# A planner's due times, allowances and forced work in a four-layer Mamba and convolution kernel

## The chip, the cores and the metric

The kernel runs on one core of one Trainium2 chip, in one launch. The metric is the device time of one execution in microseconds (us); below, the median of three runs. The core's engines work from instruction queues of their own: PE multiplies matrices (its weight loads are PEld), DVE does vector work, ACT evaluates functions, POOL does further vector work, and SP issues the DMA transfers here. All data are 32-bit floats.

## The reference

The input x is 8 images of 384 channels and 32 x 32 pixels. Four layers follow one another; each normalizes x over groups of 12 channels and adds its result to x.

```
x = x + mamba(group_norm(x))                # layer 0, "l0_"
x = x + frequency_mixer(group_norm(x))      # layer 1
x = x + mlp(mamba(layer_norm(group_norm(x))))   # layer 2, "l2_"
x = x + depthwise_3x3(group_norm(x))        # layer 3

def mamba(x):                    # per image, over 1024 pixels in order
    xin, z = split(x @ in_proj.T)               # 768 channels each
    u = silu(causal_conv3(xin))
    dt, Bm, Cm = split(u @ x_proj.T)            # 24, 16, 16 columns
    dt = softplus(dt @ dt_proj.T + bias)
    h[t] = exp(dt[t] * A) * h[t-1] + dt[t] * u[t] * Bm[t]   # 768 x 16 states
    y[t] = sum over states of h[t] * Cm[t]
    return ((y + u * D) * silu(z)) @ out_proj.T
```

Layer 1 multiplies by a 384 x 384 matrix, filters the frequencies of 8 x 8 patches, convolves 3 x 3 per channel, multiplies one half of the channels with the Gelu of the other and projects back. The mlp of layer 2 widens 384 channels to 1536, takes Gelu, and comes back.

## The kernel before

**Chunks and steps.** A Mamba layer is cut in chunks of half an image, T = 512 pixels. Layer 0 has chunks n = 0 to 15, layer 2 chunks 16 to 31; the even chunk is an image's first half (c = 0), the odd one the second. Layers 1 and 3 need both halves, so they run once per pair of chunks. A chunk has NQ = 24 steps, one for 32 of the 768 channels and their 16 states: 768 steps in all, numbered t, and i within a chunk. The loop over t (L1007) writes the engines' queues in this order for a step:

- `times` (L619, POOL) multiplies the next step's input g by B: two products of 128 x 1024.
- `scan` (L637) runs this step's four recurrences on DVE, two of them with a product by C after; POOL takes the product of the other two (L660).
- `jobs.begin` (L124) gives the step its allowance, and `jobs.step(t, 2.0)` runs a first part of the side work.
- `gather` (L664, PE) sums the states of the step before into y; every fourth step adds u * D and DVE multiplies by the gate z.
- `begin` (L610, SP) starts the load of g for the step AHEAD = 3 on; it needs that step's "dud", which the side work makes.
- `jobs.step(t)` (L133) runs more side work, and `decay` (L627) makes the next step's exp(dt * A): four matmuls into four PSUM banks, four Exp on ACT. They overwrite the banks which this step's scans read.

[...]PE comes to the next `decay` only after the side work put ahead of it, and DVE to the next scan only after the side work's DVE operations.

**Jobs.** All else is side work in generators, cut in pieces by their `yield`:

- `gates(s, h)` (L440): the gate z of half h of the channels, needed at i = 12h + 4.
- `front(s)` (L487): loads and normalizes x, in_proj, the convolution, x_proj, then dt and dud for six blocks of channels. Block 0 of the next chunk is needed at i = 21, block k at step 4k - 3 of that chunk.
- `measure(s)` (L399): group statistics of the next image, by two buffers "spm" that `front` uses too.
- `out_proj(s)` (L681): the output projection; in layer 2 it also starts the loads of the mlp's weights mw (four buffers). Called from `finish(s)` (L717), which goes on with `mlp(s)` (L891) in layer 2. Then comes `layer1` (L796) or `layer3` (L962), once per pair.

Their PSUM results go through NBANK = 3 banks (`pipe`, L189).

**The planner** (`Jobs`, L88) decides in Python, as the program is written, which piece goes where. It books a piece's PE time as columns/600 us and its DVE time as 0.1 + columns/830 us per operation (by the output's columns, L71). A job has a first step and a due step ("last"). In `step` the pieces are tried by due time, and one is put in if the step's rooms for PE and DVE (`ROOM`, L68) hold what the job's piece of that number took last time, less 0.1. A piece that ends with NEXT stops its job for this step; one that ends with EARLY stops it until `begin` of the next step, which runs one such job's next piece ahead of all else (a long Silu or Gelu). WAIT means that something isn't there yet. `begin` carries what is left of a room into the next step: at most an eighth of the room as a gain, at most the room as a debt. `until` (L148) is the force: where a step can't go on without a result, it runs pieces by due time, without regard to rooms, until the result is there. It is called for the gates (L1021), for the dud (L1035) and at the end (L1042).

Of the kernel before, what the change touches and what calls it, by code (L numbers as in the profile page):

```python
# [17 lines left out]
B, C, H, W = 8, 384, 32, 32  # L18
L = H * W
KC = C // P  # L20
# [7 lines left out]
NCH = L // T  # L28
# [12 lines left out]
NSUB = 4  # L41
NQ = ND * NSUB
QUADS = [(k, s) for k in range(ND) for s in range(NSUB)]
NH = ND // 2
# [20 lines left out]
NEXT = "next"  # L65
EARLY = "early"

ROOM = {"l0_": (5.2, 3.0), "turn": (6.4, 3.0), "l2_": (6.4, 3.0)}  # L68


class Meter:  # L71
# [18 lines left out]
class Jobs:  # L90
# [42 lines left out]
    def step(self, t, most=None):  # L133

        most = most and self.work[0] + most
        went = True
        while went and not (most and self.work[0] >= most):
            went = False
            for job in self.in_order():
                need = self.need(job)  # L140
                if job["got"] is None and job["first"] <= t and all(
                    y == 0 or x >= y - 0.1 for x, y in zip(self.room, need)
                ):
                    went = self.piece(job)
                    if went:
                        break

    def until(self, done):  # L148

        while not done():  # L150
            if not any(self.piece(job) for job in self.in_order()):
                raise RuntimeError("no job goes on")


# [1 line left out]
def tile_conv_preact_d4(ctx: ExitStack, tc: tile.TileContext, a: dict, out: bass.AP):  # L156
# [10 lines left out]
    live = {"ps": 0, "dt": 0, "x": 0, "spm": False}  # L167
    work = [0.0, 0.0]
    jobs = Jobs(work)
    vector = Meter(nc.vector, work, 1)  # L170
# [109 lines left out]
    def group_stats(block, all_read=lambda: None, between=None):  # L280
# [3 lines left out]
        for h in range(2):  # L284
            for k in range(KC):
                v, then = block(h, k)
                vector.bn_stats(st[:, k, h, :], v)
                then()
                if h == 1 and k == KC - 1:
                    all_read()  # L290
                yield between
        for k in range(KC):
            vector.bn_aggr(mv[:, k, :], _flat(st[:, k]))
        yield NEXT
# [104 lines left out]
    def measure(s):  # L399

        blocks = [(h, k) for h in range(2) for k in range(KC)]
        loaded = {}

        def load(q):
            if q < len(blocks):
                h, k = blocks[q]
                x = loaded[h, k] = wk.tile([P, T], F32, tag="spm", name="xk", bufs=2)
                nc.sync.dma_start(
                    x, s["src"][s["b"], k * P : (k + 1) * P, h * T : (h + 1) * T]
                )  # L410

        live["spm"] = True
        load(0)
        load(1)
        yield NEXT

        def block(h, k):
            return loaded.pop((h, k)), lambda: load(blocks.index((h, k)) + 2)

        def all_read():  # L420
            live["spm"] = False

        s["stats"] = yield from group_stats(block, all_read, NEXT)

# [62 lines left out]
    def front(s):  # L487

        c, n = s["c"], s["n"]
        while n > 0 and ("gates", 1) not in chunks[n - 1]:  # L490
            yield WAIT
        xn = s["xn"] = load_half(s)
        if n % (B * NCH) == 0:
# [53 lines left out]
            act(_flat(uh[h]), _flat(uh[h]), AF.Silu)  # L547
        exp_again()
        yield NEXT
        ps = yield from ps_tile("ps_x")  # L550
        for d in range(ND):
            mm(ps[:RX, :], w["x"][:, d, :], u[d], start=d == 0, stop=d == ND - 1)
# [52 lines left out]
        while flying:  # L605
            flying = [f for f in flying if next(f, f) is not f]
            yield NEXT


    def begin(s, i):  # L610
# [70 lines left out]
    def out_proj(s):  # L681
# [31 lines left out]

        yield from pipe(("ps_out", stages(m)) for m in range(KC))
        s["free"] = True

    def finish(s):  # L717

        yield from out_proj(s)
        t = NQ * s["n"]  # L720
        if s["n"] == B * NCH - 1:
            load_out(layer_w["l2_"], "l2_")
        if s["pre"] == "l2_":
            yield from mlp(s)
        s["ended"] = True
        if s["pre"] == "l2_":
            if s["c"] == NCH - 1:
                jobs.add("layer3", layer3(s), 0, t + 3 * NQ - 1)
        elif s["c"] == NCH - 1:
            until = 2 * NQ + 3 if s["n"] == B * NCH - 1 else 3 * NQ - 2  # L730
            jobs.add("layer1", layer1(s), 0, t + until)

    p2 = None

# [272 lines left out]
    for t in range(total):  # L1007
# [1 line left out]
        n = s["n"]  # L1009
        later = chunks[n + 1] if n + 1 < len(chunks) else None  # L1010
        if i == 0:
            jobs.add("gates", gates(s, 1), t + 1, t + 8)
            if s["c"] == 0 and n + NCH < len(chunks):
                jobs.add("measure", measure(chunks[n + NCH]), t, t + NQ + 4)
            if later:
                jobs.add("front%d" % (later["pre"] == "l2_"), front(later), t + 3, t + 14)
                jobs.add("gates", gates(later, 0), t + 13, t + NQ + 2)
        if i == 3 and n == B * NCH:
            load_diagonal(s["w"], s["pre"])
        if i % (NH * NSUB) == NSUB:  # L1020
            jobs.until(lambda: ("gates", i // (NH * NSUB)) in s)  # L1021
        if t + 1 < total:
            times(*steps[t + 1])
        scan(s, i)
# [2 lines left out]
        if t > 0:  # L1027
            p, q = steps[t - 1]
            gather(p, q)
            if q == NQ - 1:  # L1030
                end = 10 if p["pre"] == "l0_" else 23 if p["c"] == 0 else 16
                jobs.add("end%d" % (p["pre"] == "l2_"), finish(p), t + 1, t + end)
        if t + AHEAD < total:
            p, q = steps[t + AHEAD]
            jobs.until(lambda: p.get("dud", {}).get(QUADS[q][0]))  # L1035
            begin(p, q)
        jobs.step(t)
        if t + 1 < total:
# [134 lines left out]
```

## Time and profile before

| | |
|---|---|
| median of 3 runs | 7943.07 us (7934.12 to 7946.89) |
| the profiled execution | 7942.61 us, its span 7940.8 us |
| mean granted PE clock | 0.919 |
| busy share of PE, DVE, ACT, POOL | 92%, 72%, 51%, 71% |
| DMA | 1122.90 MB, mean 141 GB/s |
| start to first scan | 92.4 us |
| chunks 0 to 15 (layer 0) | 92.4 to 3574.4 us |
| chunks 16 to 20 | 3574.4 to 4980.2 us |
| chunks 21 to 31 | 4980.2 to 7748.3 us |
| after the last scan | 192.5 us |

Steps and chunks are read off the DVE timeline: four scans are one step, and a step lasts from its first scan to the next step's first. A busy matmul in this profile may be a waiting one (its end is modelled), so PE's share overstates its work. "Idle before" names what an engine waited for. In the table of stretches the columns are the engines' busy us with their instructions, then the granted clock, the DMA share and GB/s.

### The profile page before, as it was taken

The page shows a single profiled execution, that of the slowest core. Times are in us where ns is not written, and L with a number is a line of the kernel's source. Part 1 is how long each engine was busy: PE and PEld are TensorE (multiplying, and loading weights), DVE is VectorE, ACT ScalarE, POOL GpSimd, SP SyncE. Part 2 cuts the span into 40 slices and gives each one's busy share as a digit, 9 for nine tenths or more (in the row PEclk, how much of TensorE's full clock was granted, in tenths as well). Part 3 has the DMA queues.
Part 4 walks back from the last instruction along what each step waited for, and adds up shares of the span by engine and source line. Part 5 has one row for each costly group of instructions (what it writes and reads, how often), then busy time and mean ns, then how long its engine had stood idle before and what let it go on. Part 6 is the DMA issues. An engine that isn't in the chain of part 4 may idle for free. (4 is left out here: it accounts for less than half of the span.)

```text
span 7940.8 us, 76871 instructions
## 1 busy us (share of the span) xinstructions
PE 7334.3 (92%) x25954; PEld 3037.2 (38%) x25954; DVE 5717.7 (72%) x7254; ACT 4052.0 (51%) x6980; POOL 5639.5 (71%) x2710
## 2 busy tenths in 40 slices
PE   7989999999998999989999989999899989999898
PEld 2223333333333333333334444444444444344445
DVE  5988788878787878778737647767767676676770
ACT  4445545555555555554544545555555555555553
POOL 5888888877787878777737746767767667676770
PEclk8888888989898999989889989999999999999999
DMA  5665655555564656556526645666656666565662
GB/s 138 148 148 137 144 135 136 134 133 137 133 149 118 146 129 143 122 141 151 122 69 173 159 121 144 154 158 165 157 134 163 166 149 159 138 171 140 168 157 65
DMA packets 289704, 1122.90 MB, mean 141 GB/s; under 512 B 37402, under 2 KB 91754, under 8 KB 191004
## 3 DMA queue, kind: packets, MB, share of 16 engines
q1 hardware_dynamic: 289308, 1117.98, 57.2%
q8 instruction: 205, 3.36, 0.2%
q14 instruction: 191, 1.56, 0.1%
HBM read 1042.34 MB, written 75.50 MB: 141 GB/s over the span
## 5 line engine op out<-in xcount | busy, mean ns | idle before, releaser
L623 POOL TENSOR_TENSOR g<-g,bc 128x1024 f32<-128x1024 f32 x1536 | 3586.5, 2357 | 181.3 <-DMA g<-dud 164.4
L660 POOL TENSOR_TENSOR g<-g,bc 128x1024 f32<-128x1024 f32 x768 | 1805.8, 2351 | 1609.5 <-DVE carry L656 871.8
L241 ACT ACTIVATE dA<-dA,w_A 128x512 f32<-128x512 f32 x3072 | 1858.3, 661 | 1480.3 <-PE dA L177 1467.3
L177 PE MATMUL dA<-dt,selr 32*128 32x512 f32 x6144 | 1521.9, 676 | 67.8 <-DVE g L654 59.2
L643 DVE TENSOR_TENSOR_SCAN dA<-dA,carry,g 128x512 f32<-128x512 f32 x768 | 986.7, 1285 | 750.5 <-issue 375.4
L643 DVE TENSOR_TENSOR_SCAN dA<-dA,g 128x512 f32<-128x512 f32 x768 | 940.8, 1225 | 554.3 <-ACT dA L241 221.6
L654 DVE TENSOR_TENSOR g<-dA,bc 128x512 f32<-128x512 f32 x1536 | 1054.5, 687 | 29.8 <-DVE dA L643 0.5
L177 PE MATMUL y<-g,sely 128*32 128x512 f32 x6144 | 934.2, 640 | 47.6 <-POOL g L660 42.4
L643 DVE TENSOR_TENSOR_SCAN g<-dA,carry,g 128x512 f32<-128x512 f32 x768 | 940.4, 1266 | 0.0
L643 DVE TENSOR_TENSOR_SCAN g<-dA,g 128x512 f32<-128x512 f32 x768 | 893.7, 1206 | 0.0
L177 PEld LDWEIGHTS dA<-dt,selr 32*128 32x128 f32 x6144 | 452.1, 192 | 947.2 <-DVE g L643 473.9
L177 PE MATMUL ps_up<-t,mw 128*128 128x256 f32 x2304 | 605.4, 411 | 144.4 <-ACT h L241 100.5
L177 PE MATMUL ps_dn<-h,mw 128*128 128x256 f32 x2304 | 566.1, 397 | 67.7 <-DMA mw<-in_l_mlp_w 55.9
L177 PE MATMUL ps_z<-xf,w_in 128*128 128x512 f32 x1152 | 590.0, 653 | 27.8 <-DVE dt L85 24.0
L177 PE MATMUL ps_dw<-tp,diag 96*96 96x512 f32 x1152 | 580.7, 645 | 14.3 <-ACT diag L241 14.3
L177 PEld LDWEIGHTS ps_up<-t,mw 128*128 128x128 f32 x2304 | 444.9, 201 | 371.0 <-ACT h L241 186.7
L177 PE MATMUL ps_in<-xf,w_in 128*128 128x512 f32 x1152 | 556.2, 623 | 25.3 <-DVE u L85 22.0
L177 PE MATMUL ps_out<-u,w_out 128*128 128x512 f32 x1152 | 548.7, 623 | 9.1 <-DVE x L85 9.1
L177 PEld LDWEIGHTS ps_dn<-h,mw 128*128 128x128 f32 x2304 | 436.7, 196 | 260.3 <-issue 121.0
L177 PE MATMUL ps_dw<-xp,diag 128*128 128x512 f32 x864 | 405.4, 620 | 41.0 <-ACT diag L241 40.9
L241 ACT ACTIVATE h<-ps_up,vec 128x256 f32<-128x256 f32 x384 | 177.3, 474 | 442.7 <-PE ps_up L177 442.4
L241 ACT ACTIVATE u<-ps_in,w_vec 128x512 f32<-128x512 f32 x192 | 149.4, 778 | 478.1 <-PE ps_in L177 478.1
(98 smaller groups left out, 6514.5 us busy)
## 6 DMA issues: line engine op xcount, KB each, us to landing
g<-dud SPq DMA_DIRECT2D x768, 1024.0 KB, 7.1
mw<-in_l_mlp_w SPq DMA_DIRECT2D x384, 384.0 KB, 7.2
dud<-du SPq DMA_DIRECT2D x768, 64.0 KB, 1.7
xk<-in_x SPq DMA_DIRECT2D x48, 256.0 KB, 4.1
xf<-in_x SPq DMA_DIRECT2D x16, 768.0 KB, 8.5
x<-in_x SPq DMA_DIRECT2D x16, 768.0 KB, 8.4
x_mid<-x SPq DMA_DIRECT2D x16, 768.0 KB, 4.7
xk<-x_mid SPq DMA_DIRECT2D x48, 256.0 KB, 5.4
```

Source lines behind the costliest of these rows:

```text
L177: nc.tensor.matmul(out_, lhsT, rhs, start=start, stop=stop)
L241: nc.scalar.activation(out_, in_, func, **kw)
L623: nc.gpsimd.tensor_mul(g, g, s["bc"][:, 0, :].unsqueeze(1).to_broadcast([P, 2, T]))
L643: nc.vector.tensor_tensor_scan(dAs[j] if j < own else g[:, j, :], dAs[j], g[:, j, :], 0.0 if s["c"] == 0 else carry[:, q : q + 1], ALU.mul ...
L654: nc.vector.tensor_mul(g[:, j, :], dAs[j], s["bc"][:, 1, :])
L660: nc.gpsimd.tensor_mul(g, g, s["bc"][:, 1, :].unsqueeze(1).to_broadcast([P, 4 - own, T]))
```

## The change

All of it is in the planner and in the jobs' due times; the computation stays as it is.

- `until` takes a kind of job, and tries jobs of that kind before all others. The two forced places name what they need: "gates0" or "gates1" (two kinds now), and "front0" or "front1".
- `step` lets a piece exceed the room by 0.8 where it was 0.1. DVE's room is 2.4 for 3.0, PE's in layer 2 6.5 for 6.4.
- The output projection is a job of its own ("out0", "out1"); the rest of `finish` ("end0", "end1") is added when it is done.
- All due times are new; `measure` starts at step 11 of a chunk, not 0. Every operation of `bn_stats` is booked 0.6 us more on DVE, and of six blocks of an image's means every second one ends with NEXT, not each.
- New waits of the planner: `measure` waits for the spm buffers, `front` for its statistics and, before x_proj, for the end of the front before ("spread").

```diff
-ROOM = {"l0_": (5.2, 3.0), "turn": (6.4, 3.0), "l2_": (6.4, 3.0)}
+ROOM = {"l0_": (5.2, 2.4), "turn": (6.5, 2.4), "l2_": (6.5, 2.4)}
...
-                    y == 0 or x >= y - 0.1 for x, y in zip(self.room, need)
+                    y == 0 or x >= y - 0.8 for x, y in zip(self.room, need)
...
-    def until(self, done):
+    def until(self, done, kind=None):
         while not done():
-            if not any(self.piece(job) for job in self.in_order()):
+            late = [job for job in self.in_order() if job["kind"] == kind]
+            if not any(self.piece(job) for job in late + self.in_order()):
                 raise RuntimeError("no job goes on")
...
                 vector.bn_stats(st[:, k, h, :], v)
+                work[1] += 0.6
                 then()
...
-                yield between
+                yield between if (h * KC + k) % 2 else None
...
-        live["spm"] = True
+        while live["spm"]:
+            yield WAIT
+        live["spm"] = 2
...
-        while n > 0 and ("gates", 1) not in chunks[n - 1]:
+        while n > 0 and ("gates", 1) not in chunks[n - 1] or "stats" not in chunks[n - c]:
             yield WAIT
...
+        while n > 0 and "spread" not in chunks[n - 1]:
+            yield WAIT
         ps = yield from ps_tile("ps_x")
...
         s["free"] = True
+        jobs.add("end%d" % last, finish(s), 0, NQ * (s["n"] + 1) + 18)

     def finish(s):
-        yield from out_proj(s)
...
-                jobs.add("layer3", layer3(s), 0, t + 3 * NQ - 1)
+                jobs.add("layer3", layer3(s), 0, t + 2 * NQ + 14)
         elif s["c"] == NCH - 1:
-            until = 2 * NQ + 3 if s["n"] == B * NCH - 1 else 3 * NQ - 2
-            jobs.add("layer1", layer1(s), 0, t + until)
+            jobs.add("layer1", layer1(s), 0, t + NQ + 8)
...
         if i == 0:
-            jobs.add("gates", gates(s, 1), t + 1, t + 8)
-            if s["c"] == 0 and n + NCH < len(chunks):
-                jobs.add("measure", measure(chunks[n + NCH]), t, t + NQ + 4)
+            jobs.add("gates1", gates(s, 1), t + 1, t + 4)
             if later:
-                jobs.add("front%d" % (later["pre"] == "l2_"), front(later), t + 3, t + 14)
-                jobs.add("gates", gates(later, 0), t + 13, t + NQ + 2)
+                jobs.add("front%d" % (later["pre"] == "l2_"), front(later), t + 2, t + 6)
+                jobs.add("gates0", gates(later, 0), t + 13, t + NQ - 3)
+        if i == 11 and s["c"] == 0 and n + NCH < len(chunks):
+            jobs.add("measure", measure(chunks[n + NCH]), t, t + 1)
...
         if i % (NH * NSUB) == NSUB:
-            jobs.until(lambda: ("gates", i // (NH * NSUB)) in s)
+            h = i // (NH * NSUB)
+            jobs.until(lambda: ("gates", h) in s, "gates%d" % h)
...
             if q == NQ - 1:
-                end = 10 if p["pre"] == "l0_" else 23 if p["c"] == 0 else 16
-                jobs.add("end%d" % (p["pre"] == "l2_"), finish(p), t + 1, t + end)
+                jobs.add("out%d" % (p["pre"] == "l2_"), out_proj(p), t + 1, t + 3)
...
-            jobs.until(lambda: p.get("dud", {}).get(QUADS[q][0]))
+            jobs.until(
+                lambda: p.get("dud", {}).get(QUADS[q][0]), "front%d" % (p["pre"] == "l2_")
+            )
...
-    jobs.add("end1", finish(steps[-1][0]), 0, total)
+    jobs.add("out1", out_proj(steps[-1][0]), 0, total)
```

More of the change, by code (lines that the diff above doesn't have):

```diff
@@ L165, in tile_conv_preact_d4 @@
     psy = ctx.enter_context(tc.tile_pool(name="psy", bufs=1, space=PSUM))
-    live = {"ps": 0, "dt": 0, "x": 0, "spm": False}
+    live = {"ps": 0, "dt": 0, "x": 0, "spm": 0}
     work = [0.0, 0.0]
@@ L420, in all_read @@
         def all_read():
-            live["spm"] = False
+            live["spm"] = 0
         s["stats"] = yield from group_stats(block, all_read, NEXT)
@@ L607, in front @@
             yield NEXT
+        s["spread"] = True
     def begin(s, i):
```

## The prediction

> **What bounds the kernel now.** I read the page first, for the engines' shares.
>
> ```profile
> PE 7334.3 (92%) x25954; PEld 3037.2 (38%) x25954; DVE 5717.7 (72%) x7254; ACT 4052.0 (51%) x6980; POOL 5639.5 (71%) x2710
> ...
> PEclk8888888989898999989889989999999999999999
> ...
> L623 POOL TENSOR_TENSOR g<-g,bc 128x1024 f32<-128x1024 f32 x1536 | 3586.5, 2357 | 181.3 <-DMA g<-dud 164.4
> L660 POOL TENSOR_TENSOR g<-g,bc 128x1024 f32<-128x1024 f32 x768 | 1805.8, 2351 | 1609.5 <-DVE carry L656 871.8
> ```
>
> PE looks full, but a "busy" matmul may be one that stands waiting. POOL owes every scan step three products, 3 x 2.35 = 7.1 us: a step's floor. For PE's real need I use the chain of waits, where 36 half-records of ps_dw (18 matmuls of 512 columns) take 15.72 us, 0.87 us each; the planner books 512/600 = 0.85. Below, "PE" amounts are in those booked us. In the timeline the four dA matmuls of a step take 1.14 us, the four y 1.06, D 1.13 every fourth step: 2.3 PE per step besides the jobs.
>
> Second, the busy time in stretches, one per chunk (24 steps): chunks 12, 13, 17, 20, 22, 23.
>
> ```profile
> 2676.30:2908.60 232.30, 220.25 (x750) 75.31 (x749) 184.38 (x270) 115.47 (x218) 175.25 (x88) 0.93 0.54 130
> 2908.60:3116.60 208.00, 194.23 (x669) 71.44 (x668) 171.78 (x182) 120.02 (x214) 176.68 (x83) 0.91 0.60 144
> 3817.20:4149.60 332.40, 305.59 (x906) 117.76 (x905) 179.23 (x193) 160.05 (x306) 175.96 (x84) 0.89 0.39 95
> 4667.30:4980.20 312.90, 281.92 (x1091) 145.81 (x1090) 185.21 (x270) 150.95 (x247) 176.68 (x88) 0.94 0.57 147
> 5230.40:5490.40 260.00, 241.37 (x913) 108.74 (x912) 180.58 (x266) 142.40 (x240) 175.41 (x87) 0.97 0.59 148
> 5490.40:5740.70 250.30, 225.32 (x918) 112.34 (x918) 175.82 (x192) 125.80 (x204) 176.99 (x85) 0.95 0.64 162
> ```
>
> Columns: stretch, length, busy us of PE, weight loads, DVE, ACT, POOL, granted clock. DVE and POOL need 172 to 185 us in every chunk; the length above that comes from PE. Layer 0 owes 64,512 matmul columns of job work per chunk (its half of layer 1 included), 107.5 PE, so (107.5 + 24 x 2.3)/0.92 = 177 us: PE and POOL level. Layer 2 owes 88,576 columns, 147.6 PE, so (147.6 + 55)/0.955 = 212 us: PE bounds it.
>
> Third, the DVE timeline of the longest step (chunk 17, step 21).
>
> ```profile
> 4006.17 2.45 DVE L643 TENSOR_TENSOR_SCAN g<-dA,carry,g 128x512 f32<-128x512 f32 x2
> 4022.46 0.69 DVE L85 TENSOR_TENSOR gate<-ps_dw,gate 96x512 f32<-96x512 f32 x1 [13.84 <-PE ps_dw L177]
> ...
> 4066.15 0.69 DVE L85 TENSOR_TENSOR gate<-ps_dw,gate 96x512 f32<-96x512 f32 x1 [29.94 <-PE ps_dw L177]
> ...
> 4128.80 0.69 DVE L85 SCALAR_TENSOR_TENSOR dt<-ps_dt,spm 128x512 f32<-128x512 f32 x1 [14.38 <-ACT spm L241]
> ...
> 4131.22 1.29 DVE L643 TENSOR_TENSOR_SCAN dA<-dA,carry,g 128x512 f32<-128x512 f32 x1
> ```
>
> No scan starts for 123 us: until (L148) forces the front's first dud, and all of layer 1 and an output projection, due earlier, go first. Between first scans the step is 128.9 us. Adding the planner's prices, 102 PE are in it: (102 + 2.3)/0.89 = 117. So a forced lump is mostly honest PE work, 12 us dearer than that. Smaller ones: 33.4 us (21.3 PE) at step 21 of chunks 12 and 14, 37.0 in 16, 70.3 before step 4 of chunk 20, 35.4 there in 22, 24 ... 30.
>
> Fourth, PE outside lumps, in chunk 23.
>
> ```profile
> 5623.17 1.07 PE L177 MATMUL y<-g,sely 128*32 128x512 f32 x8
> 5629.00 5.44 PE L177 MATMUL ps_up<-t,mw 128*128 128x256 f32 x12 [4.76 <-ACT h L241]
> ```
>
> PE stands 4.76 us while ACT does two table loads of 1.28 us and a long Silu. Such events leave chunk 23 at 250 us where (137.4 + 55)/0.95 = 203 would do.
>
> **What the Trainium skill says.** "Perfetto Trace Analysis", Identifying the Most-Contended Engine: matmul busy share is no measure of closeness to the limit. The trace agrees: 225 us busy for a need of 203 in chunk 23. "TensorE: Matmul & The Clock Gate", Part 1, Architectural detail: ACT and DVE queues are strictly first in, first out. The lumps agree: the next scan sits behind the forced evictions. "ScalarE: Activation LUTs", What ACT_TABLE_LOAD costs: 1283 ns a load; the trace has 1283. No page bears on the planner.
>
> **The change part by part.** No matmul, activation, scan or weight is added; the order changes. The new waits are the planner's (spread, stats, spm), so no engine queues behind them. What moves on SP's queue: x (768 KB, 8.4 us) and four mw loads (7.2 us each) with the projection, and measure's six xk (4 to 5 us) from steps 0-10 to 11-14. They pass g loads, issued three steps (25 us) ahead and landing in 7.1: hidden; uncovered, at most 8 us per chunk. Two statistics per step cost DVE 2 x 0.68 instead of one, in three steps instead of six: zero in sum. Layer statistics, six in one step before (booked 0.11 each, really 0.68; that step took 13.3 us in chunk 12), now spread: 1 to 2 us per pair, inside the rounding.
>
> *Layer 0.* I follow the new dues by hand. Even chunk: projection (15.4 PE), gates1 (7.7), front (27.3), done about step 14; layer 1's patches, one stage a step (NEXT), about step 9 to step 2 of the odd chunk. Odd chunk: layer 1 is overdue, so first: its depthwise part, 72 PE at two 2.56 pieces a step, fills steps 3 to 19 (before, it did this in steps 1-16 of the even chunk). The projection gets in at its two EARLY gaps, gates1 is forced at 16, and the front begins its matmuls at step 20 and is forced at 21 with some 19 PE: the 33.4 us lump again, in the other chunk. "Forced alone" doesn't help, it was alone in chunk 12 too. So every pair looks like chunks 12+13: 232.3 + 208.0 = 440.3 us, against a mean for chunks 2 to 15 of (3574.4 - 490.0)/7 = 440.6. Priced by classes of steps from before (up to 2 PE 7.5 us, 2 to 4.2 8.45, about 5.1 9.1, the lump 31) my list gives 449. I take 0 for layer 0; ends -60 and +60.
>
> What does change: all 215 PE of each pair are done within it. Before, chunks 0-15 did 1537 PE; the new order does 100.7 + 7 x 215 = 1606. Some 70 fewer are owed at the turn.
>
> *The turn, chunks 16 to 20.* Before: 4980.2 - 3574.4 = 1405.8 us with 762 job PE. Following the dues: chunk 16 does 90 (latency-bound), 17 134, 18 to 20 154 each at the room's pace: 686, leaving the same owed after chunk 20. (686 + 5 x 55)/0.93 = 1033, plus 45 us of stalls a chunk (what chunks 21-30 show on average is 40) = 225, plus 25 because chunk 16 is at POOL's floor: 1283. I take -120. Gates forced alone are evicted by ACT, not DVE, so scans aren't behind them.
>
> *Layer 2 steady, chunks 21 on.* Room 6.5 and slack 0.8 make steps of three 2.56 pieces (7.68) and two (5.12) alternate. The even chunks' 35.4 us lump goes, but it held 25.6 + 5.1 + 2.3 = 33 PE: nothing is gained by spreading it. By classes of before, 7 to 8 PE cost a median 12.7 us, 5.12 9.1: ten heavy and fourteen light give 254.4, against a mean of 254.4 for chunks 21 to 30. I take 0; ends -90 and +110.
>
> *Tail.* 192.5 us, with 22 PE of the previous pair's layer 3 leading it; that fits before the end now: -22/0.95 = -23, -3 of gaps in its chain, +18 paid in spare room earlier: -8.
>
> Sum on the profiled 7940.8 (92.4 to the first scan unchanged): 0 - 120 + 0 - 8 = 7813; the run has 2 us more outside the span, and its 7942.61 is the median's 7943.07 within 0.5: 7815.
>
> **The rivals.** *Smoothing pays.* In layer 2 the two-piece front steps take 9.2 us because DVE (6.2 scan + 2.9 taps) ends last, PE idling 1.5; a third piece rides free. Heavy steps at 11.5: 115 + 14 x 9.42 (class mean) = 247, -7.5 x 11 chunks = -82, and 4 us per layer 0 pair from the earlier x load (DVE stood 9.10 us for x in step 316): 7705. Against: steps of 7 to 8 PE took a median 12.7 before.
>
> *Heavy steps stall: slower.* The third piece needs one of three PSUM banks, whose evictions stand behind ACT's Gelu and Silu (4.76 us above; PE waited 88.2 us for h in 4400:7748). At 14.0 us a heavy step, a chunk is 140 + 132 = 272, +17.5 x 11 = +192: 8007. It decides from 13.4 us on: (254.4 + 128/11 - 131.9)/10.
>
> *It does nothing.* Lumps in seven odd chunks of layer 0 (the +60 end) and front lumps in 17 to 19 of the old size give back the turn: 7935.
>
> **How the numbers follow.** Forecast 0.42 (own range 7760 to 7870), smoothing 0.28, heavy steps 0.20, nothing 0.10. A measurement of this kernel tells 0.2% (16 us). Faster: 0.42 + 0.28 + 0.02 of the last; same 0.06; slower 0.20 + 0.02. Range 7640 to 7985: smoothing's centre less its unknown (-65), up to most of the +110 and +60 ends together; the far part of heavy steps stays out.
>
> **What would show it.** Right: no gap over 60 us between scans; chunks 16-20 near 1285 us; no 35 us lump at step 3 of even layer 2 chunks; a lump of some 30 us at step 21 of odd layer 0 chunks. Wrong: layer 0 pairs off 440 by over 10, or layer 2 pairs off 509 by over 15.

## The result and the profile after

The changed kernel takes 8043.76 us (median of 4 runs, 8024.73 to 8049.89) against 7944.98 us before (median of four runs now): a ratio of 1.0121, with a 95% interval of 1.01 to 1.0143. It is slower by some 1.2%. The forecast was 7815 us, in a range of 7640 to 7985. The profiled execution took 8049.89 us, its span 8048.1 us at a mean granted clock of 0.912, against 7940.8 us at 0.919: 107.3 us more.

| stretch (first scan to first scan) | before | after | difference | forecast |
|---|---|---|---|---|
| start, and chunks 0 and 1 | 490.0 | 498.2 | +8.2 | 0 |
| chunks 2 to 15 | 3084.4 | 3136.8 | +52.4 | 0 |
| chunks 16 to 20 (the turn) | 1405.8 | 1288.7 | -117.1 | -120 |
| chunks 21 to 30 | 2543.4 | 2717.0 | +173.6 | 0 |
| chunk 31 | 224.6 | 234.0 | +9.4 | +18, here or earlier |
| after the last scan | 192.6 | 173.3 | -19.3 | -26 |

The forecast's -8 for the tail is -26 at the end and +18 for the same work paid earlier; the two measured rows give -9.9. So the turn and the tail did what was forecast. The loss lies in layer 2's steady part, and a smaller one in layer 0. The page of the kernel after, by the same lines as before (the code has moved: L623 is L630 now, L660 is L667, L643 is L650):

```profile
PE 7281.8 (90%) x25954; PEld 3030.2 (38%) x25954; DVE 5765.3 (72%) x7254; ACT 4045.9 (50%) x6980; POOL 5633.0 (70%) x2710
...
PEclk8789989898989999898889999998989999999999
...
L630 POOL TENSOR_TENSOR g<-g,bc 128x1024 f32<-128x1024 f32 x1536 | 3581.8, 2353 | 173.4 <-DMA g<-dud 148.8
L667 POOL TENSOR_TENSOR g<-g,bc 128x1024 f32<-128x1024 f32 x768 | 1803.9, 2349 | 1803.9 <-DVE g L650 963.1
```

The instructions are the same in number on every engine, and POOL's products last as long as before. PE is busy for 53 us less in a span that is 107 us longer, so it stands idle more. The busy time in stretches of the kernel after, chunks 12, 13, 17, 20, 22 and 23 as before, and then chunks 2 to 15, 16 to 20 and 21 to 30 (columns as in the prediction: length, busy us of PE, weight loads, DVE, ACT, POOL, granted clock, and then DMA share and GB/s):

```profile
2733.80:2951.60 217.80, 202.13 (x712) 78.19 (x712) 190.77 (x272) 120.01 (x208) 179.94 (x95) 0.89 0.61 147
2951.60:3174.20 222.60, 210.11 (x706) 68.42 (x705) 171.01 (x179) 116.11 (x224) 172.04 (x76) 0.95 0.52 126
3859.80:4129.90 270.10, 247.45 (x767) 86.95 (x766) 173.12 (x182) 131.81 (x246) 175.94 (x78) 0.89 0.48 115
4655.00:4923.80 268.80, 241.40 (x948) 121.08 (x945) 179.56 (x265) 128.77 (x204) 178.12 (x89) 0.91 0.60 155
5190.90:5466.30 275.40, 246.55 (x994) 128.85 (x993) 179.53 (x265) 127.41 (x199) 178.89 (x89) 0.91 0.63 159
5466.30:5731.20 264.90, 237.93 (x891) 105.41 (x891) 179.75 (x197) 142.82 (x248) 172.89 (x82) 0.94 0.55 139
498.20:3635.00 3136.80, 2922.36 (x9914) 1037.45 (x9910) 2541.07 (x3154) 1649.38 (x3007) 2459.90 (x1181) 0.91 0.56 134
3635.00:4923.80 1288.80, 1169.87 (x4318) 523.28 (x4317) 906.16 (x1181) 655.34 (x1106) 880.61 (x427) 0.91 0.58 145
4923.80:7640.80 2717.00, 2403.57 (x9221) 1143.79 (x9221) 1781.37 (x2276) 1355.77 (x2227) 1767.82 (x847) 0.93 0.58 146
```

The last three stretches in the kernel before:

```profile
490.00:3574.40 3084.40, 2924.42 (x9739) 1032.04 (x9736) 2483.98 (x3148) 1628.03 (x2930) 2464.30 (x1184) 0.90 0.57 136
3574.40:4980.20 1405.80, 1285.31 (x4531) 565.88 (x4530) 907.70 (x1190) 693.22 (x1197) 882.08 (x426) 0.92 0.54 135
4980.20:7523.70 2543.50, 2331.67 (x9114) 1103.02 (x9113) 1777.37 (x2272) 1339.80 (x2208) 1761.70 (x843) 0.96 0.62 155
```

In chunks 21 to 30 the length less PE's busy time is 211.8 us before and 313.4 us after: 102 us more of idling. PE's busy time rises by 72 us as well, for 1% more records; the granted clock there falls from 0.96 to 0.93. DVE and POOL are as busy as before. So the 173 us show on PE: it waits more, and it is busy longer for nearly the same work.

The longest step of the kernel before, 128.9 us, was in chunk 17, step 21. The DVE timeline of the same step of the kernel after:

```profile
4079.93 2.95 DVE L85 SCALAR_TENSOR_TENSOR u<-ps_in,w_vec,u 128x511 f32<-128x511 f32 x4
4086.95 1.53 DVE L85 SCALAR_TENSOR_TENSOR u<-ps_in,w_vec,u 128x511 f32<-128x511 f32 x2 [4.07 <-ACT xt L242]
...
4105.21 0.69 DVE L85 SCALAR_TENSOR_TENSOR dt<-ps_dt,spm 128x512 f32<-128x512 f32 x1 [14.09 <-ACT spm L242]
...
4107.62 1.29 DVE L650 TENSOR_TENSOR_SCAN dA<-dA,carry,g 128x512 f32<-128x512 f32 x1
```

Only the front itself is forced now, and the step takes 33.9 us. The work that made the long step isn't gone: the planner put layer 1 and the projection into earlier steps. What that is worth at the turn, a_layer1_late measures below. The PE timeline of chunk 23, step 7, where a step of the steady part took 19.8 us:

```profile
5541.99 1.56 PE L178 MATMUL ps_up<-t,mw 128*128 128x256 f32 x6
5551.37 5.49 PE L178 MATMUL ps_up<-t,mw 128*128 128x256 f32 x12 [7.82 <-ACT h L242]
5556.79 1.23 PE L178 MATMUL y<-g,sely 128*32 128x512 f32 x8
5557.95 2.86 PE L178 MATMUL ps_up<-t,mw 128*128 128x256 f32 x12
```

PE stands 7.82 us because ACT does two table loads, the gates' long Silu and layer 3's xp and diag before it comes to the h that frees a bank. Then twelve ps_up records take 5.49 us; a little later twelve of the same take 2.86. The granted clock was 0.50 for the first twelve:

```profile
5546.90:5557.20 10.30, 5.83 (x16) 4.08 (x20) 2.23 (x2) 5.18 (x10) 6.95 (x3) 0.50 0.12 38
```

This idle stretch is paid for twice. The Trainium skill, "TensorE: Matmul & The Clock Gate", Why this matters for your kernels, says that gaps of more than some 3 us between matmul bursts throw the clock back to half; these records agree with it. The last section shows where the clock fell without such a gap. In chunks 21 to 30, PE has 26 idle stretches of over 3 us before (101.6 us in all) and 41 after (191.7 us).

### The profile page after: what moved, and what is told of

Read it like the earlier page. It is cut to its first block, busy times and chain, and to the rows that moved or that the text cites. A ratio compares the mean times of both kernels' runs of the same rounds, so it can differ in the third digit from the quotient of the medians.

```text
span 8048.1 us, 76877 instructions
## 1 busy us (share of the span) xinstructions
PE 7281.8 (90%) x25954; PEld 3030.2 (38%) x25954; DVE 5765.3 (72%) x7254; ACT 4045.9 (50%) x6980; POOL 5633.0 (70%) x2710
## 5 line engine op out<-in xcount | busy, mean ns | idle before, releaser
L630 POOL TENSOR_TENSOR g<-g,bc 128x1024 f32<-128x1024 f32 x1536 | 3581.8, 2353 | 173.4 <-DMA g<-dud 148.8
L667 POOL TENSOR_TENSOR g<-g,bc 128x1024 f32<-128x1024 f32 x768 | 1803.9, 2349 | 1803.9 <-DVE g L650 963.1
L650 DVE TENSOR_TENSOR_SCAN dA<-dA,carry,g 128x512 f32<-128x512 f32 x768 | 986.9, 1285 | 730.0 <-issue 309.0
L178 PE MATMUL dA<-dt,selr 32*128 32x512 f32 x6144 | 1432.3, 692 | 58.9 <-DVE g L661 55.3
L650 DVE TENSOR_TENSOR_SCAN dA<-dA,g 128x512 f32<-128x512 f32 x768 | 939.9, 1224 | 707.0 <-ACT dA L242 267.5
L650 DVE TENSOR_TENSOR_SCAN g<-dA,carry,g 128x512 f32<-128x512 f32 x768 | 940.3, 1266 | 0.0
L650 DVE TENSOR_TENSOR_SCAN g<-dA,g 128x512 f32<-128x512 f32 x768 | 893.6, 1206 | 0.0
L178 PEld LDWEIGHTS dA<-dt,selr 32*128 32x128 f32 x6144 | 428.1, 196 | 892.7 <-DVE g L650 401.8
L178 PE MATMUL ps_in<-xf,w_in 128*128 128x512 f32 x1152 | 583.5, 648 | 52.5 <-DVE u L85 50.3
L178 PE MATMUL ps_dw<-tp,diag 96*96 96x512 f32 x1152 | 546.9, 612 | 9.4 <-ACT diag L242 9.4
L178 PE MATMUL ps_dw<-xp,diag 128*128 128x512 f32 x864 | 431.0, 643 | 61.1 <-ACT diag L242 52.6
L178 PEld LDWEIGHTS y<-g,sely 128*32 128x32 f32 x6144 | 133.2, 110 | 682.4 <-issue 414.6
```

Source lines behind the costliest of these rows:

```text
L178: nc.tensor.matmul(out_, lhsT, rhs, start=start, stop=stop)
L630: nc.gpsimd.tensor_mul(g, g, s["bc"][:, 0, :].unsqueeze(1).to_broadcast([P, 2, T]))
L650: nc.vector.tensor_tensor_scan(dAs[j] if j < own else g[:, j, :], dAs[j], g[:, j, :], 0.0 if s["c"] == 0 else carry[:, q : q + 1], ALU.mul ...
L667: nc.gpsimd.tensor_mul(g, g, s["bc"][:, 1, :].unsqueeze(1).to_broadcast([P, 4 - own, T]))
```

## The experiments

The amounts called "booked PE" are the planner's own: matmul columns over 600 for the pieces that it put into the steps. Names with a_ are edits of the kernel after, names with b_ edits of the kernel before. Each ratio is to executions of the kernel before taken beside it. The runs by stretch, from the one profiled execution of each (us; booked PE of chunks 21 to 30 in the last column):

| kernel | median, ratio to before | 2 to 15 | 16 to 20 | 21 to 30 | chunk 31 and tail | booked |
|---|---|---|---|---|---|---|
| before | 7944.98 | 3084.4 | 1405.8 | 2543.4 | 417.2 | 1476 |
| after | 8043.76, 1.0121 | 3136.8 | 1288.7 | 2717.0 | 407.3 | 1503 |
| b_slack | 7835.96, 0.9864 | 2991.3 | 1342.4 | 2585.6 | 417.5 | 1475 |
| a_slack_l0 | 7938.43, 1.0001 | 3143.3 | 1270.1 | 2557.4 | 469.9 | 1461 |
| a_means_l2 | 7961.00, 1.0022 | 3143.1 | 1220.4 | 2688.9 | 405.4 | 1501 |
| a_layer1_late | 8000.22, 1.0077 | 3002.1 | 1376.7 | 2707.7 | 406.2 | 1503 |
| a_old_dues | 8009.15, 1.0085 | 3128.7 | 1372.2 | 2583.0 | 415.2 | 1492 |
| a_layer3_late | 8169.33, 1.0283 | 3130.5 | 1294.4 | 2798.0 | 438.6 | 1484 |
| a_old_rooms | 8070.32, 1.0165 | 3169.0 | 1249.8 | 2701.3 | 435.1 | 1482 |
| a_old_front | 7952.71, 1.0001 | 3174.3 | 1223.9 | 2651.8 | 407.7 | 1504 |
| a_old_ends | 7917.42, 0.9968 | 3167.8 | 1268.3 | 2546.2 | 436.1 | 1476 |
| a_old_front_ends | 8005.50, 1.0073 | 3253.6 | 1251.8 | 2558.1 | 442.7 | 1477 |
| a_old_end | 8067.12, 1.0149 | 3142.9 | 1296.6 | 2696.1 | 438.0 | 1479 |
| a_old_out | 7889.41, 0.9920 | 3171.1 | 1266.4 | 2544.9 | 410.7 | 1503 |
| a_old_ends_layer1 | 7861.20, 0.9889 | 3045.7 | 1342.7 | 2545.7 | 439.6 | 1476 |
| b_force | 8145.76, 1.0248 | 3078.0 | 1380.4 | 2730.1 | 468.6 | 1476 |
| b_slack_force | 7779.23, 0.9794 | 2970.5 | 1294.7 | 2567.8 | 438.6 | 1474 |

How far such a stretch repeats can be read from the table: after, a_slack_l0, a_means_l2, a_layer3_late and a_old_end have the same pieces in the same steps of layer 0, and took 3130.5 to 3143.3 us; after and a_layer1_late have the same in chunks 21 to 30, and took 2717.0 and 2707.7. A difference of some 13 us tells nothing.

### Slack, means and layer 1

The first theory was the rival of the prediction that came nearest to the measured time: heavy steps (three pieces), which slack 0.8 makes, stall. Its opponent was that the order of the jobs costs, and slack little. The slack alone, in the kernel before:

```
-                    y == 0 or x >= y - 0.1 for x, y in zip(self.room, need)
+                    y == 0 or x >= y - 0.8 for x, y in zip(self.room, need)
```

> The kernel before with the slack of the rooms at 0.8 instead of 0.1 and nothing else. By the planner's arithmetic, chunks 21 to 30 then hold 75 steps of more than 7 PE (10 before, 87 in the changed kernel), no forced lump at step 3, and layer 2's due times and the means stay as before. Theory 'heavy steps stall' (a third 2.56 piece in a step is what costs): chunks 21 to 30 take about 2690 us instead of 2543 (75/87 of the +173 measured). Theory 'order' (the new due times put the gates and the output projection where the mlp's pieces meet their Silu, and the means where they meet the layer norm): they take 2520 to 2560. The turn (chunks 16 to 20) has 744 PE for 762 and its forced lump 58 for 99: about 1370 us either way. Layer 0 (chunks 2 to 15) within 30 us of 3084.

Chunks 21 to 30 took 2585.6 us, 42 more than before at the same booked work, with 75 heavy steps for 10: outside both ranges, nearer to the second. Layer 0 won 93 us, which neither theory had. The whole is faster by 1.4% (0.9864, interval 0.9845 to 0.9884). So slack alone isn't the loss, and heavy steps as such are not: they lasted 11.46 us on average.

The slack taken back in the kernel after, from chunk 17 on:

```
-                    y == 0 or x >= y - 0.8 for x, y in zip(self.room, need)
+                    y == 0 or x >= y - self.slack for x, y in zip(self.room, need)
...
+        jobs.slack = 0.8 if n <= B * NCH else 0.1
         jobs.begin(ROOM
```

> The changed kernel with the slack back at 0.1 from chunk 17 on, 0.8 kept in layer 0. Steps of more than 7 PE in chunks 21 to 30 fall from 87 to 9; the work that no longer fits is forced instead, 8 to 24 PE at step 21 of every chunk, and 40 PE less is done before chunk 31. Heavy steps: chunks 21 to 30 fall from 2717 to 2560-2600 us (40 PE less alone is worth 42 us), the end grows by about 50 us. Order: they stay above 2660.

Chunks 21 to 30 fell by 160 us, as the first theory had it. The planner books 42 PE less there, work that comes back at the end (63 us more after the start of chunk 31), so about 115 us are more than that. Slack 0.8 costs 42 us in the old order and more than twice that in the new one: slack and order act together, and each theory has a part of the truth.

The means of a batch at their old place, in layer 2 only (from step 0 of the even chunk, one block a step):

```
-        if i == 11 and s["c"] == 0 and n + NCH < len(chunks):
-            jobs.add("measure", measure(chunks[n + NCH]), t, t + 1)
+        if i == (11 if n < B * NCH else 0) and s["c"] == 0 and n + NCH < len(chunks):
+            jobs.add("measure", measure(chunks[n + NCH]), t, t + (1 if n < B * NCH else NQ + 4))
...
-                yield between if (h * KC + k) % 2 else None
+                yield between if (h * KC + k) % 2 or late() else None
```

> The changed kernel, but in layer 2 the means of a batch start at step 0 and take one block a step, as before. In even chunks of layer 2 the layer norm then no longer shares the two buffers with them: in chunks 22 and 24 its variance ran three steps late and PE stood 8.47 us for it in one step. If the means' new place costs: chunks 21 to 30 fall by 40 to 80 us. If heavy steps or the other due times cost: by less than 25.

(`late()` holds once layer 2 has its first statistics.) At nearly the same booked work, the turn is 68 us shorter and chunks 21 to 30 are 28 us shorter, which lies between the two theories. The new place and pace of the means cost some 96 us in this order, where the prediction had put zero; a_old_out below keeps them and has no loss in chunks 21 to 30. Why they cost stays open: in chunks 21 to 30 PE's waits for the layer norm's ps_lv fell from 50.5 to 36.0 us, but those for h rose from 53.7 to 76.3.

Layer 1 due a chunk later, but for the last pair:

```
-            jobs.add("layer1", layer1(s), 0, t + NQ + 8)
+            jobs.add("layer1", layer1(s), 0, t + (NQ + 8 if s["n"] == B * NCH - 1 else 2 * NQ + 8))
```

> The changed kernel with layer 1's due time one chunk later in layer 0 (56 instead of 32 steps past its pair's last chunk's start; the last pair keeps 32). By the planner's arithmetic layer 0 does 1538 PE instead of 1606, as the kernel before did, and the turn has 751 with one forced lump of 101 PE. My account of the change (layer 0 pays for the work that the turn is spared): chunks 2 to 15 fall from 3137 to about 3090 us, chunks 16 to 20 rise from 1289 to about 1390, chunks 21 to 30 stay within 20 us of 2717. Rival (the turn's gain comes from its own due times and from forcing the late job alone): the turn stays under 1330.

Chunks 2 to 15 fell by 135 us, more than expected, with 68 PE less booked in layer 0 (1538 for 1606; at a clock of 0.91 that is 75 us). The turn, which then owes that work, rose by 88 us, with the lump of chunk 17 back (127.1 us). So layer 1's early due time moves work from the turn into layer 0: 88 of the turn's 117 us are gained so, and layer 0 pays 135 for them, a net 47 us.

### Due times

What slack and means leave open is which new due time costs in layer 2. All the old ones, put back into the kernel after:

```
-            jobs.add("gates1", gates(s, 1), t + 1, t + 4)
+            jobs.add("gates1", gates(s, 1), t + 1, t + 8)
-                jobs.add("front%d" % (later["pre"] == "l2_"), front(later), t + 2, t + 6)
-                jobs.add("gates0", gates(later, 0), t + 13, t + NQ - 3)
+                jobs.add("front%d" % (later["pre"] == "l2_"), front(later), t + 3, t + 14)
+                jobs.add("gates0", gates(later, 0), t + 13, t + NQ + 2)
```

and in the same way the projection and the end (both at t + 10, 16 or 23 of the next chunk), layer1 and layer3.

> The kernel after, with every due time of the kernel before (second-half gates, front, first-half gates, projection out and end, layer1, layer3); slack 0.8, rooms, places of the means and the forcing by kind stay. Booked TensorE us of the planner: layer 0 1538 (after 1606), chunks 16-20 751 (683), 21-30 1492 (1503), last chunk and tail 266 (255). Due-time theory (what is left of the loss in layer 2, and the loss in layer 0, comes from which jobs now run side by side): layer 0 near 3000 us, chunks 16-20 near 1380 (the gates of chunk 17 are forced in one lump of 100 us), chunks 21-30 between 2600 and 2640; the whole 7900 to 7940 us. Rival, rooms and slack: chunks 21-30 stay at 2690 to 2710, since heavy steps (83 against 87) and slack are as in the kernel after; the whole near 8000 us.

Chunks 21 to 30 fell by 134 us for 11 PE less of work: the due-time theory holds there, the rival doesn't. In layer 0 it missed: 3128.7 us, not 3000, with lumps of up to 24 PE forced in step 21 of the even chunks 8 to 16. Layer 3's due time alone:

```
-                jobs.add("layer3", layer3(s), 0, t + 2 * NQ + 14)
+                jobs.add("layer3", layer3(s), 0, t + 3 * NQ - 1)
```

> The kernel after, with only layer3's due time back at the old one (step 23 of the following even chunk's pair end, in place of step 14 of the odd chunk). Booked TensorE us: layer 0 1606, chunks 16-20 673, 21-30 1484 (after 1503), tail 285 (255). Bank-sharing theory (layer3's pieces alternate with front pieces whose results VectorE takes out late): chunks 21-30 fall from 2717 to 2620 to 2660, more than the 19 us of work that moves; the whole near 7990 us. Rival (layer3 isn't the cause): chunks 21-30 between 2690 and 2705, tail up by 30, the whole within 8035 to 8060 us.

Both expectations failed: chunks 21 to 30 rose by 81 us. A layer 3 that runs beside the front isn't the cause; the new, earlier due time of layer 3 helps in this order. The rooms of before:

```
-ROOM = {"l0_": (5.2, 2.4), "turn": (6.5, 2.4), "l2_": (6.5, 2.4)}
+ROOM = {"l0_": (5.2, 3.0), "turn": (6.4, 3.0), "l2_": (6.4, 3.0)}
```

> The kernel after with the rooms of before (TensorE 6.4 in place of 6.5 in layer 2, VectorE 3.0 in place of 2.4 everywhere). Booked TensorE us: layer 0 1606, chunks 16-20 680, 21-30 1482 (after 1503), tail 279 (255); heavy steps 79 against 87. Room theory (the tenth of room fills steps that the scan had left free, or less VectorE room bunches the pieces): chunks 21-30 fall to 2640 to 2670 us. Rival (rooms only shift work to the end): 2690 to 2700, tail up by 25 us, the whole within 8040 to 8060 us.

Chunks 21 to 30 fell by 16 us, less than the 21 PE that move away, and the end took 28 us more: the rival's case. The front's due time alone (the front line of the long diff above), and those of projection and end:

```
-                jobs.add("out%d" % (p["pre"] == "l2_"), out_proj(p), t + 1, t + 3)
+                jobs.add("out%d" % (p["pre"] == "l2_"), out_proj(p), t + 1, t + (10 if p["pre"] == "l0_" else 23 if p["c"] == 0 else 16))
...
-        jobs.add("end%d" % last, finish(s), 0, NQ * (s["n"] + 1) + 18)
+        jobs.add("end%d" % last, finish(s), 0, NQ * (s["n"] + 1) + (10 if s["pre"] == "l0_" else 23 if s["c"] == 0 else 16))
```

> The kernel after with the front's old first step and due time alone (from step 3, due in step 14, in place of step 2 and 6). Booked TensorE us: layer 0 1606 as after, chunks 16-20 683 as after, 21-30 1504 (after 1503), tail 254; heavy steps 79 (87). Front theory (of the old due times together, which took 134 us off chunks 21-30, it is the front's, which keeps its pieces out of the steps of the MLP half): chunks 21-30 between 2600 and 2640 us, layer 0 about as after, the whole 7940 to 7980 us. Rival (it is the projection's and the end's due times): chunks 21-30 between 2690 and 2720, the whole 8030 to 8060 us.

> The kernel after with the old due times of projection out and end alone (both in step 10 of the next chunk in layer 0, 16 or 23 in layer 2, in place of step 3 for the projection and 18 for the end). Booked TensorE us: layer 0 1584 (after 1606), chunks 16-20 705 (683; the gates of chunk 17 forced in a lump of 41 us), 21-30 1476 (1503), tail 281 (255); heavy steps 65 (87). Theory of projection and end: chunks 21-30 between 2580 and 2620 us, more than the 27 us of work that moves to the tail; the whole 7950 to 8000 us. Rival (the front's due time): chunks 21-30 between 2680 and 2700, tail up by 25, the whole 8040 to 8070 us.

The front gives 65 us, between the two theories. Projection and end give 171 us, nearly all of the loss, with 27 PE less booked. Both together:

> The kernel after with the old due times of front, projection out and end together (gates, layer1 and layer3 keep the new ones). Booked TensorE us: layer 0 1606, chunks 16-20 683, 21-30 1477, tail 281, no forced lump in layer 2. If the two due times act together: chunks 21-30 below 2600 us and layer 0 still near 3140 (lumps of 19 us in step 21 of its odd chunks), the whole near 7930 us. Rival (each acts alone): chunks 21-30 equal to the better one of the two single edits.

Chunks 21 to 30 are no better than with projection and end alone (2558.1 and 2546.2 us). Layer 0 missed its expectation by over 110 us, at 3253.6; why the old front due time is so dear there stays open. Then the two due times apart, the end's (second half of the diff) and the projection's (first half):

> The kernel after with the old due time of the end alone (residual, MLP half and statistics: step 16 or 23 of the next chunk in layer 2 in place of step 18; 10 in layer 0), the projection's new one kept. Booked TensorE us: layer 0 1606 as after, chunks 16-20 683 as after, 21-30 1479 (after 1503), tail 280 (255). End theory (the end's pieces and the front's alternate because the end is due after the front): chunks 21-30 between 2550 and 2600 us. Projection theory (putting the projection ahead of everything brings the end's pieces beside the front's): chunks 21-30 between 2670 and 2700. Layer 0 near 3140 in both.

> The kernel after with the old due time of the projection alone (step 16 or 23 of the next chunk in layer 2, 10 in layer 0, in place of step 3), the end's new one kept. Booked TensorE us: layer 0 1584, chunks 16-20 705, 21-30 1503 and tail 255 as after. Projection theory: chunks 21-30 between 2560 and 2610 us at the work of the kernel after. End theory: 2690 to 2720. Layer 0 near 3165 in both (its lumps in step 21 are up to 24).

Of the two it is the projection's. With the end's old due time, 24 PE less and 21 us less: only the work. With the projection's, the same 1503 PE and 172 us less. The stretch of chunks 21 to 30 in that kernel:

```profile
4935.40:7480.30 2544.90, 2339.53 (x9225) 1115.53 (x9225) 1776.84 (x2274) 1350.97 (x2225) 1768.47 (x846) 0.96 0.62 156
```

9225 records as against 9221: the work is the same, and the order differs. PE idles 205.4 us instead of 313.4, and its busy time is 64 us less at a clock of 0.96 for 0.93. Its idle stretches of over 3 us are 20 (79.0 us) instead of 41 (191.7 us). Steps of 7 to 9 PE last 11.27 us on average (75 of them) where they lasted 12.57 (87 of them). PE's waits in that stretch, first of the kernel after (total us, times, longest):

```profile
PE ps_up L178 <- ACT h L242: 53.7, 43, 7.8
PE ps_lv L178 <- ACT sq L242: 50.5, 10, 8.6
PE ps_dw L178 <- ACT diag L242: 40.8, 16, 4.6
PE ps_dn L178 <- DMA mw<-in_l_mlp_w: 37.8, 16, 6.4
PE ps_in L178 <- DVE u L85: 36.3, 17, 4.9
PE ps_up L178 <- DMA mw<-in_l_mlp_w: 34.7, 14, 6.2
```

and of a_old_out:

```profile
PE ps_dn L178 <- DMA mw<-in_l_mlp_w: 51.9, 21, 5.2
PE ps_lv L178 <- ACT sq L242: 34.7, 10, 8.6
PE ps_up L178 <- ACT h L242: 29.9, 38, 5.0
PE ps_dw L178 <- ACT diag L242: 20.8, 11, 4.6
...
PE ps_up L178 <- DMA mw<-in_l_mlp_w: 6.7, 5, 3.5
...
PE ps_in L178 <- DVE u L85: 4.8, 12, 0.6
```

The gain isn't in one wait: the banks that DVE and ACT empty (ps_in, ps_up) come free sooner, and what ACT makes for PE (diag for ps_dw, sq for ps_lv) and the mlp's first weights (for ps_up) are there sooner; only the wait for the second weights (ps_dn) grew. In the planner's account the order differs by this: with the projection due in step 3 it goes ahead of the second half of the gates, which ends in step 6.9 of a chunk on average in place of 4.9. The next front waits for those gates, so it begins two steps later, and the rest falls behind it. That the loss goes when the projection's due time goes back is shown. That the later front is the link is not: a_old_end, whose gates end still later (step 8.0), keeps the loss, but a_slack_l0 (step 12.2) does not, nor does a_old_dues (step 6.4). Nor is the due time the only cause. Four single edits take something off chunks 21 to 30 without taking a like amount of work: the projection's due time 172 us, the slack 160 (for 42 PE), the front's due time 65 and the means 28. They come to far more than the loss of 173.6, so what they take off overlaps.

The table has the same division by the projection throughout: of the kernels with slack 0.8, the seven with the projection due first took 2652 to 2798 us in chunks 21 to 30, the seven with its old due time 2545 to 2586.

Last, the two edits that gave most, together:

> The kernel after with the old due times of projection and end, and layer1 due a chunk later as in the run on layer1 (the last pair keeps the new one): the two edits that gave most. Booked TensorE us: layer 0 1549 (old ends alone 1584), chunks 16-20 740 (705; a lump of 85 us in chunk 17), 21-30 1476 and tail 281 as with the old ends alone. If the causes in layer 0 and layer 2 are separate: layer 0 near 3020 (3168 with the old ends alone), chunks 16-20 near 1360, 21-30 2546, the whole 7840 to 7880 us, below the kernel before and above 7779. If layer 0's loss is not layer1's due time but lumps and more work: layer 0 3100 or more, the whole above 7920 us.

The layer 0 stretch of a_old_ends:

```profile
497.80:3665.50 3167.70, 3007.50 (x9865) 1066.00 (x9865) 2526.00 (x3148) 1649.86 (x2993) 2460.50 (x1180) 0.90 0.55 133
```

and of a_old_ends_layer1:

```profile
498.70:3544.40 3045.70, 2888.49 (x9782) 1023.59 (x9782) 2487.39 (x3148) 1634.64 (x2954) 2463.68 (x1184) 0.90 0.58 138
```

Layer 0 fell by 122 us for 35 PE less (39 us at a clock of 0.90), short of the expected 148; the turn rose by 74 us, and chunks 21 to 30 stayed where they were. The causes in layers 0 and 2 are separate, and layer 1's due time is worth more than layer 0's whole loss of 52 us.

### Forcing

The forcing by kind alone in the kernel before, and with slack 0.8:

```
-    def until(self, done):
+    def until(self, done, kind=None):
...
-            if not any(self.piece(job) for job in self.in_order()):
+            late = [job for job in self.in_order() if job["kind"] == kind]
+            if not any(self.piece(job) for job in late + self.in_order()):
```

> The kernel before with the forcing of the awaited job first as its only edit (slack 0.1). Booked TensorE us: layer 0 1538 as before, chunks 16-20 715 (before 762; no lump of 55 us in chunk 20), 21-30 1476 as before but its lumps of 31 us in step 3 of the even chunks give way to ones of 33 us in step 21, last chunk and tail 319 (271). If forcing pays by itself: chunks 16-20 near 1320 (before 1406), chunks 21-30 as before, tail up by 45: the whole 7880 to 7910 us, ratio 0.992 to 0.996. Rival (it pays only with slack 0.8, whose schedule leaves few lumps): chunks 16-20 gain what the tail loses, the whole 7930 to 7960 us.

> The kernel before with two edits of the change only: slack 0.8, and the forcing of the awaited job first. Booked TensorE us: layer 0 1565 as with slack alone, chunks 16-20 724 (slack alone 744), 21-30 1474 (1475), last chunk and tail 284 (264). If lumps matter (the forced lump of chunk 17 is one of 58 us and those of chunks 19 and 20, 15 and 23 us, are gone): chunks 16-20 between 1300 and 1325 against 1342, tail 195 against 176, the whole 7820 to 7840 us. Rival, forcing alone leaves more work behind and shifts it: nothing gained in chunks 16-20, tail up, the whole 7850 to 7880 us.

By itself the forcing makes the kernel slower by 2.5% (1.0248, interval 1.0225 to 1.0271), which neither expectation had: step 21 of the even chunks from 22 on gets lumps of 33 PE, and takes 50 us. Chunks 21 to 30 lose 187 us at the old booked work, and the end 51 for 47 PE more. With slack 0.8 the same edit takes 57 us off the kernel with slack alone, 48 of them at the turn; the only step over 20 us left is chunk 17's. The three stretches of that kernel, the fastest here:

```profile
501.00:3471.50 2970.50, 2867.34 (x9818) 1014.69 (x9818) 2505.50 (x3149) 1644.30 (x2976) 2463.58 (x1184) 0.93 0.60 142
3471.50:4766.10 1294.60, 1190.11 (x4414) 528.99 (x4413) 906.96 (x1186) 660.45 (x1137) 878.73 (x424) 0.94 0.58 144
4766.10:7333.90 2567.80, 2327.21 (x9103) 1102.03 (x9102) 1778.46 (x2272) 1333.13 (x2209) 1760.06 (x842) 0.95 0.61 153
```

It has the turn of the kernel after (1294.6 us) without its layer 2, and a layer 0 that is 114 us shorter than before: 7779.23 us, a ratio of 0.9794 (interval 0.9767 to 0.9822). It beats both kernels.

## Why the prediction was wrong

**Layer 2, "I take 0; ends -90 and +110": the step that failed.** It measured +173.6 us, outside its own ends. The working took a chunk for ten heavy steps at 12.7 us and fourteen light ones of 5.12 PE at 9.1, and so priced a step by the PE amount in it. Two things were wrong with that.

The steps were others. Of the 240 in chunks 21 to 30, 87 held 7 to 9 PE and took 12.57 us on average, 72 held 5.3 to 7 and took 11.06, 67 held about 5.1 and took 9.76; 12 were smaller, and two were lumps of 11 PE. The class from 5.3 to 7 was there in the kernel before, 90 steps at 10.73 us, and the working has no place for it; the 9.1 of the light class is its median, its mean is 9.42. An estimate from the class means of the kernel before (10.0, 9.42, 10.73 and 12.59 us; the two lumps as measured) gives 2665 us for these steps, 121 of the 173.6 us.

And a step's size doesn't set its price. The same means give 2626 us for the steps of a_old_out, 39 less than for the kernel after. It measured 172 less, 2544.9 us. Which jobs share a step, and so what PE waits for, moved more here than the amounts did. The prediction read the order from the due times, and used it only to count amounts.

**Layer 0, "I take 0 for layer 0".** Its own list gave 449 us a pair and was set aside for the 440.3 of chunks 12 and 13. The seven pairs took 448.1 us on average (3136.8/7). Chunks 12 and 13 came as worked out, 440.4 us. The loss is in the first pairs: chunks 2 and 3 took 446.6 us for 421.8, chunks 4 and 5 446.9 for 432.1, with 210 and 215 PE booked for 179 and 195. The mean of 440.6 before was one of pairs that put work off. The 68 PE that layer 0 takes over from the turn were credited there and charged nowhere. The lumps in step 21 of the odd chunks came, with 11 to 14 forced PE for the 19 worked out: 23.6 to 26.8 us in chunks 3 to 13, and 35.0 in 15.

**The turn, "I take -120".** -117.1 us, with 683 PE booked for the 686 worked out, and no step above 34 us in it. That it came so close is partly luck: a_means_l2 books the 686 itself and took 1220 us, 63 us below the 1283 worked out, so the means put at zero made up for a sum that was too high.

**The means, "zero in sum".** DVE's work is the same, but their place and pace cost 68 us of the turn and 28 of chunks 21 to 30, as a_means_l2 shows. **The tail, -8.** Its mechanism is right: -19.3 us at the end for the -26, and +9.4 in chunk 31 for the +18, -9.9 together.

**The rivals.** "Heavy steps stall" named 8007 us, nearest to the result. Its price isn't borne out: it decides from 13.4 us a heavy step on, these lasted 12.57, and with slack alone 75 of them came at 42 us. But a_slack_l0 shows that in the new order the slack that makes them costs some 115. "Smoothing pays" asked for cheap third pieces in layer 2; b_slack has them there, and loses 42 us. Its 93 us of gain are in layer 0, where only 4 steps hold more than 7 PE; what brings them is not shown. All four signs named for "right" came, the lumps a little smaller; only the pairs of layer 2 (543 us against 509) told the failure.

## What to carry to other kernels

Judge a schedule by what the bounding engine waits for in each stretch, not by the amounts in its steps: here one due time moved 172 us at equal work. Before a mean is used as a forecast, look at what went into it: the pairs of layer 0 did unlike work. Edits to this planner don't add up: forcing alone lost 2.5%, and gained 0.7% on top of the slack. Work moved out of a crowded stretch is only won if the stretch that takes it is charged for it.

## What the runs showed of the hardware

PE's longer busy time is the granted clock's. In chunks 21 to 30, busy time times mean granted clock is nearly the same in four kernels: 2331.6 us at 0.958 before, 2403.6 at 0.928 after, 2339.5 at 0.957 in a_old_out and 2468.2 at 0.908 in b_force, which gives 2234, 2231, 2239 and 2241. The clock's records in these traces have two values, 1.0 and 0.5.

Long idle stretches go with half the clock. In the kernel after, 37 of the 41 idle stretches of over 3 us in chunks 21 to 30 have a stretch at half clock that begins in them or within 7 us of their end. But these are only 37 of its 70 stretches at half clock. In b_force the clock is lower still, with 50 us more idling than before (261.9 for 211.8) and 137 us more busy time:

```profile
4949.90:7680.00 2730.10, 2468.24 (x9113) 1143.74 (x9112) 1782.90 (x2271) 1342.93 (x2208) 1761.22 (x842) 0.91 0.58 144
```

Its ten longest stretches at half clock, five of 27.3 and five of 17.1 us, all lie in step 21, where the front is forced, and no idle stretch of over 3 us is in them or in the 7 us before. The first of them, and three lines of its PE timeline:

```profile
5192.60:5219.90 27.30, 22.97 (x54) 8.79 (x54) 14.91 (x16) 13.09 (x22) 17.57 (x9) 0.50 0.41 96
...
5197.09 1.21 PE L178 MATMUL ps_dt<-dbc,w_dt 25*128 25x512 f32 x1 [2.73 <-DVE dt L85]
5198.11 2.75 PE L178 MATMUL dA<-dt,selr 32*128 32x512 f32 x5
5203.89 1.94 PE L178 MATMUL y<-g,sely 128*32 128x512 f32 x8
```

PE is busy for 23.0 of the 27.3 us; eight y records take 1.94 us, for 1.06 in the kernel before. So the sum of idling doesn't tell the clock: a_slack_l0, which has ten such stretches in its forced steps too, idles 200.8 us, less than the kernel before, at a granted clock of 0.932. What holds the clock down there, the short waits or the small matmuls, no run separates.
